# First image of a convolution and attention block: x loaded ahead of the raw taps, BatchNorm factors on VectorE, third buffer for the last output pieces

## The chip, the cores and the metric

One core of a Trainium2 chip runs the whole program. Its engines are named as in the profile: PE (TensorE, matrix products; PEld its weight loads), DVE (VectorE), ACT (ScalarE), POOL (GpSimd) and SP (SyncE, which here issues most of the DMA loads; POOL issues the stores). The metric is the device time of one execution in microseconds (us). A time within the program is given from the start of the profiled span.

## The reference

The input x has 8 images of 512 channels by 32 x 32 points, in 32-bit floats. Each image is normalised over 32 groups of channels, goes through a block, and is added to the block's output:

```python
def cbs(x, w, p, pad):
    return silu(bn_eval(conv2d(x, w, pad), p))     # bn: (x - m) * g / sqrt(v + 1e-3) + b

t = cbs(gn(x), cv1_w, cv1_bn, 0)                   # 512 -> 512, 1 x 1
ys = [t[:, :C], t[:, C:]]                          # C = 256
for i in range(2):
    yi = ys[-1]
    z = cbs(yi, m_cv1_w[i], m_cv1_bn[i], 1)        # 256 -> 256, 3 x 3
    z = bot_attention(z, m_qkv_w[i], m_rw[i], m_rh[i])   # 4 heads of 64 over 1024 points
    z = silu(bn_eval(conv2d(z, m_cv2_w[i], 0), m_cv2_bn[i]))
    ys.append(yi + z)
out = x + cbs(concat(ys, axis=1), cv2_w, cv2_bn, 0)
```

## The kernel before

Channels lie on the 128 partitions, in chunks of 128; the 1024 points of an image lie along the free axis and are worked on in two halves of 512. The images go one after another. From the second image on, the normalisation and cv1 of an image are done beside the attention of the image before it. The first image has nothing to hide behind: the part of the program ahead of the loop over `b` (L1271 to L1324) prepares it, and this is where most of the change lies.

That part does the following. SP's queue loads, in this order, chunk 0 of x, the raw 3 x 3 taps of the first convolution for output chunk 0 and input chunk 0 (`load_raw`, L153), chunk 1 of x, the first half of cv1's weights, chunks 2 and 3 of x, the second half of those weights, and then further raw taps and the BatchNorm parameters `bnp` (L205).

DVE takes statistics of the four chunks of x (`gn_stats`, L486 to L490). The group norm is made for chunks 0 and 1 and for chunks 2 and 3 apart (`group_norm_part`, L520): two small products on PE average over groups (`gm_ps`, `gv_ps`, L497), DVE makes the deviation (L506 to L509) and adds epsilon (L516), POOL raises to the power -0.5 and makes the shift (L517, L532, L533), and ACT applies scale and shift to x in place (L537). As chunks of x become ready, PE runs the products of cv1 (L387). Its four output chunks are taken in the order `Y_ORDER` = 2, 3, 0, 1; those of `ypad` (2 and 3) are the input of the first 3 x 3 convolution.

The 3 x 3 convolution is done by transforms: rows and columns of the input are transformed into `v_in` (`tiles_in`, L392 to L446, on DVE), the taps into `u` (`make_u`, L322 to L346, on DVE with copies on ACT), PE multiplies (L971), and DVE and ACT transform back (`columns_out`, L450; `rows_out`, L459). There are three transforms `i` = 0, 1, 2 of the taps for every pair of output chunk and input chunk `k`. For the first image the taps' transforms are made from the raw taps and also stored to memory for later images (L1318, L1268).

The factors of all BatchNorms are made in one go from `bnp`, 16 columns a partition: `rstd` = (variance + epsilon) to the power -0.5, `sh` = weight times `rstd`, `bh` = bias minus mean times `sh`, and two columns pairs of `sh` scaled by -1/12 (L1304 to L1311). All of this runs on POOL. Every SiLU (L370, on ACT) reads `sh` and `bh`.

The order of instructions on an engine is made when the program is built: a scheduler places each instruction by its own estimates of when its inputs are ready and by the order in the source. `tc.issue_after(ins)` asks that what is recorded inside it is not placed before `ins`. Each engine works through its list strictly in order.

At the end of the program, `cv2` (L1206) makes the last image's output, chunk by chunk. An output piece is a tile `t`: DVE adds an earlier partial product to PE's result (L1236), ACT applies SiLU, DVE adds the input x (L1239), and a DMA stores it (L1241). The last output chunk is cut into pieces of 512, 256 and 256 points, whose tiles have the tags "t", "h", "h"; each tag is a ring of two buffers, shared with other tiles of that tag. The tag "wt" is that of temporary tiles in `tiles_in` (L427).

Of the kernel before, what the change touches and what calls it, by code (L numbers as in the profile page):

```python
# [44 lines left out]
F32 = mybir.dt.float32  # L45
I32 = mybir.dt.int32
AF = mybir.ActivationFunctionType
ALU = mybir.AluOpType
# [4 lines left out]
P = 128  # L53
BN_EPS = 1e-3
# [7 lines left out]
def kernel(  # L62
# [16 lines left out]
    nc = tc.nc  # L79
# [4 lines left out]
    NX = C1 // P  # L84
    NM = C // P
# [12 lines left out]
    act = fast.enter_context(tc.tile_pool(name="act", bufs=1))  # L98


    def load_x(pool, b, c, bufs):
        xt = pool.tile([P, HW], F32, tag="x", name="x", bufs=bufs)
        src = x[b, ts(c, P), :] if isinstance(b, int) else x[bass.ds(b, 1), ts(c, P), :][0]
        nc.sync.dma_start(xt, src)
        return xt

    xs = [load_x(act, 0, 0, NX)]


    def ring(shape, name):  # L110
# [9 lines left out]
    def load_w1_half(i):  # L120
        ks = slice(i * NX // 2, (i + 1) * NX // 2)
        nc.sync.dma_start(w1[:, ks], cv1_w.rearrange("(k p) o -> p k o", p=P)[:, ks])
# [13 lines left out]
    def load_raw(n, oc, k, tag, bufs=1):  # L136
        raw = act.tile([P, 9, P], F32, tag=tag, name="raw", bufs=bufs)
        nc.sync.dma_start(raw, m_cv1_w[n, ts(k, P), :, ts(oc, P)])
        return rows_of_raw(raw)
# [11 lines left out]
        return rows_of_raw(raw[:, 0:9]), (both, mid)  # L151

    raws = {(0, 0, 0): load_raw(0, 0, 0, "k")}  # L153
    xs.append(load_x(act, 0, 1, NX))
    load_w1_half(0)
    xs += [load_x(act, 0, c, NX) for c in range(NX // 2, NX)]

# [40 lines left out]
    bnp = const.tile([P, NBN, 4], F32, name="bnp")  # L198
# [108 lines left out]
    sh = const.tile([P, NBN], F32, name="sh")  # L307
    bh = const.tile([P, NBN], F32, name="bh")
    rstd = const.tile([P, NBN], F32, name="rstd")
# [6 lines left out]
    def new_u(name):  # L316
        return ring([P, NM, 2, NC, P], name)
# [4 lines left out]
    def make_u(i, u, raw):  # L322


        rows, g1 = raw
        g0, g2 = rows[:, 0], rows[:, 1]
        stt, tt = nc.vector.scalar_tensor_tensor, nc.vector.tensor_tensor
        a, b = u[:, 0, 0:3], u[:, 1, 0:3]
        plus, minus = u[:, :, 1], u[:, :, 3]
        if i == 2:  # L330
            nc.scalar.copy(u[:, :, 0:3:2], rows[:, :, 0::2])
            tt(minus, rows[:, :, 0], rows[:, :, 2], ALU.add)
            tt(plus, minus, rows[:, :, 1], ALU.add)
            return tt(minus, minus, rows[:, :, 1], ALU.subtract)
        if i == 0:
            tt(b, g0, g2, ALU.add)
            tt(a, b, g1, ALU.add)
            tt(b, b, g1, ALU.subtract)
        else:
            stt(b, g2, 4.0, g0, ALU.mult, ALU.add)  # L340
            stt(a, g1, 2.0, b, ALU.mult, ALU.add)
            stt(b, g1, -2.0, b, ALU.mult, ALU.add)

        tt(minus, u[:, :, 0], u[:, :, 2], ALU.add)
        tt(plus, minus, plus, ALU.add)
        return stt(minus, minus, 2.0, plus, ALU.mult, ALU.subtract)  # L346
# [18 lines left out]
    def stages(act, small, ps_big, ps_av, n_pt):  # L365


        def silu(dst, src, k):

            return nc.scalar.activation(dst, src, AF.Silu, scale=sh[:, k : k + 1], bias=bh[:, k : k + 1])  # L370
# [635 lines left out]
        def cv2_products(w2, ys, oc, ks, ps=None, ends=None, by_half=False):  # L1006
            def cat(k, half):
                part, c = divmod(k, NM)
                if part in (1, 2):
                    return inner(ys[part], c, half)  # L1010
                return ys[part][:, c, ts(half, HALF)]

            nk = (2 + N) * NM
            return conv1x1(lambda k: w2[2 * k // nk][:, k % (nk // 2), ts(oc, P)], cat, nk, ks, ps, ends, by_half)
# [191 lines left out]
        def cv2(b, w2, ys, begun={}, parts={}):  # L1206

            def rows_of(dram, oc, at, n):  # L1210
                if isinstance(b, int):
                    return dram[b, ts(oc, P), at : at + n]
                return dram[bass.ds(b, 1), ts(oc, P), at : at + n][0]

            def residual(oc):
                t = act.tile([P, HW], F32, tag="xr", name="x_res", bufs=2)
                nc.gpsimd.dma_start(t, rows_of(x, oc, 0, HW))
                return t

            res = [residual(oc) for oc in range(2)]  # L1220
            for oc in range(NO):
                ks = range((2 + N) * NM)
                if oc in begun:
                    ps = cv2_products(w2, ys, oc, ks[-NM:], begun[oc], by_half=oc == NO - 1)
                else:
                    ks = ks[2 * NM if oc in parts else 0 :]
                    ps = cv2_products(w2, ys, oc, ks, ends=(ks[0], ks[-1]), by_half=oc == NO - 1)
                final = isinstance(b, int) and oc == NO - 1
                sizes = (HALF, HALF // 2, HALF // 2) if final else (HALF, HALF)
                x_res = res.pop(0)  # L1230
                at = 0
                for n, size in enumerate(sizes):
                    t = act.tile([P, size], F32, tag="h" if n and final else "t", name="t", bufs=2)
                    src = ps[:, at // HALF, at % HALF : at % HALF + size]
                    if oc in parts:
                        nc.vector.tensor_tensor(t, src, parts[oc][:, at : at + size], ALU.add)  # L1236
                        src = t
                    silu(t, src, bn_cv2 + oc)
                    nc.vector.tensor_tensor(t, t, x_res[:, at : at + size], ALU.add)  # L1239
                    q = nc.sync if final else nc.gpsimd  # L1240
                    q.dma_start(rows_of(out, oc, at, size), t)  # L1241
                    at += size
                if oc + 2 < NO:
                    res.append(residual(oc + 2))
# [26 lines left out]
    loaded = s.table_of(AF.Silu)  # L1271
    u_first = [new_u("u_new") for _ in range(PAIRS)]
# [3 lines left out]
    Y_ORDER = [*Y1S, *Y0S]  # L1276
    _, _, (_, read, _, _) = s.group_norm_part(xs[: NX // 2])
    norm = s.group_norm_part(xs[NX // 2 :])
    with tc.issue_after(loaded.ins):
        made = make_u(2, u_first[2][:, 0], raws[0, 0, 0])  # L1280
    with tc.issue_after(read.ins):
        next(norm)
    with tc.issue_after(made.ins):
        made = make_u(0, u_first[0][:, 0], raws[0, 0, 0])
    begun = {}

    def begin(oc, ks):
        begun[oc] = s.cv1_products(w1, xs, oc, ks, begun.get(oc))
        return s.last_product[0]
# [4 lines left out]
    with tc.issue_after(averaged.ins):  # L1294
        made = make_u(1, u_first[1][:, 0], raws[0, 0, 0])
    begin(Y_ORDER[0], [1])
    first = begin(Y_ORDER[1], [0])
    with tc.issue_after(first.ins):
        multiplied, _, applied, shifted = next(norm)
    with tc.issue_after(multiplied.ins):  # L1300
        begin(Y_ORDER[1], [1])
        begin(Y_ORDER[2], range(NX // 2))
    with tc.issue_after(shifted.ins):
        nc.gpsimd.tensor_scalar(rstd, bnp[:, :, 3], BN_EPS, None, ALU.add)  # L1304
        nc.gpsimd.tensor_tensor(rstd, rstd, mhalf[:, :NBN], ALU.pow)
        nc.gpsimd.tensor_tensor(sh, bnp[:, :, 0], rstd, ALU.mult)
        nc.gpsimd.tensor_tensor(bh, bnp[:, :, 2], sh, ALU.mult)
        nc.gpsimd.tensor_tensor(bh, bnp[:, :, 1], bh, ALU.subtract)

        for at in bn_m1:  # L1310
            nc.gpsimd.tensor_scalar(sh[:, at : at + NM], sh[:, at : at + NM], -1 / 12, None, ALU.mult)  # L1311
    with tc.issue_after(made.ins):
        made = make_u(0, u_first[0][:, 1], raws[0, 0, 1])
    with tc.issue_after(made.ins), tc.issue_after(applied.ins):
        for i in (1, 2):
            made = make_u(i, u_first[i][:, 1], raws[0, 0, 1])
    for i in range(PAIRS):
        nc.gpsimd.dma_start(u_dram[0][0][i], u_first[i])  # L1318
    last = made
# [6 lines left out]
    for b in range(B):  # L1326
# [6 lines left out]
        def u_of(n):  # L1333
            def of(oc):
                nonlocal last_load
                if b == 0 and n == 0 and oc == 1:
                    with tc.issue_after(last.ins):
                        for i in range(PAIRS):
                            make(n, oc, [i])
                got = [us.pop((oc, i)) if (oc, i) in us else load_u(n, oc, i) for i in range(PAIRS)]  # L1340
                if (b > 0 or n > 0) and oc == 1:
                    sq[n], last_load = load_sq(n)
                return got

            return of


        z, t = s.conv3x3(0, vs, u_of(0), b > 0)
# [4 lines left out]
        if more:  # L1353

            with tc.issue_after(last_load.ins) if last_load else nullcontext():
                xs = [load_x(act, b + 1, c, NX) for c in range(NX)]
# [60 lines left out]
        made = None  # L1417
        if b == 0:
            made = make(1, 1, [1], place=act.tile([P, NM, 2, NC, P], F32, tag="q", name="u_new"))
        with tc.issue_after(made.ins) if made else nullcontext():  # L1420
            last = s.m2(0, ao, y1, lambda oc, half: inner(y2, oc, half))
# [12 lines left out]
        z, t = s.conv3x3(1, vs, u_of(1), True)  # L1434
# [50 lines left out]
        last = s.m2(1, ao, y2, lambda oc, half: ylast[:, oc, ts(half, HALF)])  # L1485
# [103 lines left out]
```

## Time and profile before

| | us |
|---|---|
| median of 4 runs (lowest to highest) | 2319.03 (2318.39 to 2319.87) |
| the profiled execution: its own time | 2318.68 |
| the profiled execution: span from first to last instruction | 2317.2 |
| busy in the span: PE | 2288.7 (99%) |
| busy: DVE | 1838.6 (79%) |
| busy: ACT | 987.4 (43%) |
| busy: POOL | 94.7 (4%) |
| mean granted clock of PE | 0.997 |

A line of the timeline gives the start, the duration, the engine, the source line, the operation, the tile written and the tiles read, the sizes, how many instructions are merged, and in brackets the idle time of the engine before it and what released it. A line of the waits gives who waited for whom, the total, the number of waits and the longest. Instructions of DVE that do not depend on one another start before the one ahead has quite ended; so a stream of 128 x 256 operations advances by 0.34 us an operation, one of 128 x 384 by 0.47, although one alone takes 0.41 and 0.55. A PE product of 32-bit floats appears as two matmul records.

### The profile page before, as it was taken

To read this page: it belongs to the slowest core of one execution; us is meant where nothing else is said; L and a number is where in the kernel's file an instruction comes from. 1 tells how busy PE (TensorE), PEld (TensorE's weight loads), DVE (VectorE), ACT (ScalarE), POOL (GpSimd) and SP (SyncE) were. 2 spreads that over 40 slices of the span, in tenths; PEclk is the share of its full clock that TensorE was granted. 3 is DMA by queue.
4 is the path that set the end of the run, shared out by engine and by line. 5 is a ranking of instruction groups with operands and counts; after the bars stand their busy time and mean duration, and the time that the engine had idled before them with its cause. 6 is when DMAs were issued, how large, how long until landed. Compare 5 with 4: busy or idle time off the path is not lost.

```text
span 2317.2 us, 36534 instructions
## 1 busy us (share of the span) xinstructions
PE 2288.7 (99%) x14806; PEld 1174.2 (51%) x14806; DVE 1838.6 (79%) x2914; ACT 987.4 (43%) x1292; POOL 94.7 (4%) x314
## 2 busy tenths in 40 slices
PE   7999999999999999999999999999999999999998
PEld 4547346463554636446364553645436364473643
DVE  7887977888788887888788887888877988777774
ACT  2443624536144352544525345253542535335352
POOL 2000000000000000000000000000000000000000
PEclk9999999999999999999999999999999999999999
DMA  7422334041430415213151221602216031260201
GB/s 242 170 86 87 108 112 186 16 150 34 145 142 15 150 34 190 102 37 124 51 221 53 70 93 50 250 29 94 67 47 250 29 128 33 68 228 15 87 11 62
DMA packets 95521, 235.60 MB, mean 102 GB/s; under 512 B 28016, under 2 KB 50736, under 8 KB 81904
## 3 DMA queue, kind: packets, MB, share of 16 engines
q1 hardware_dynamic: 83600, 182.84, 23.5%
q0 software_dynamic: 11744, 50.34, 5.7%
q8 instruction: 119, 1.95, 0.4%
q14 instruction: 58, 0.48, 0.1%
HBM read 198.54 MB, written 34.60 MB: 101 GB/s over the span
## 4 chain that ended last, share of the span: by engine, by line
PE 96%; DVE 3%; POOL 0%; ACT 0%; DMA 0%; issue 0%; SPq 0%; DVEq 0%; POOLq 0%; ACTq 0%
PE av_ps L769 19%; PE l_ps L735 19%; PE c_ps L971 14%; PE c L1029 8%; PE p_ps L631 8%; PE x_ps L1141 6%; PE c_new L1029 6%; PE m_ps L995 5%; PE ps L387 4%; PE pv_ps L635 3%; PE s_ps L787 1%; PE p_ps L635 1%; PE s_ps L805 1%; DVE acc L755 0%; DMA raw<-in_m_cv_w_dram 0%; PE v_ps L596 0%
## 5 line engine op out<-in xcount | busy, mean ns | idle before, releaser
L739 ACT ACTIVATE pt<-l_ps 128x1024 f32<-128x1024 f32 x512 | 494.9, 1023 | 410.1 <-PE l_ps L735 385.6
L755 DVE TENSOR_TENSOR acc<-acc,pt 128x1024 f32<-128x1024 f32 x384 | 469.4, 1222 | 65.6 <-ACT pt L739 39.8
L769 PE MATMUL av_ps<-pt,vT 64*64 64x512 f32 x4096 | 486.5, 592 | 0.5 <-DVE ao L777 0.5
L735 PE MATMUL l_ps<-q,kr 64*64 64x512 f32 x4096 | 486.0, 590 | 0.0
L971 PEld LDWEIGHTS c_ps<-v_in,u 128*128 128x128 f32 x2720 | 306.0, 192 | 6.7 <-issue 6.7
L971 PE MATMUL c_ps<-v_in,u 128*128 128x128 f32 x2720 | 306.2, 275 | 0.0
L769 PEld LDWEIGHTS av_ps<-pt,vT 64*64 64x64 f32 x4096 | 159.2, 133 | 269.4 <-issue 224.3
L735 PEld LDWEIGHTS l_ps<-q,kr 64*64 64x64 f32 x4096 | 160.1, 133 | 263.3 <-issue 252.1
L453 ACT COPY m<-c_ps 128x256 f32<-128x256 f32 x96 | 35.4, 368 | 220.3 <-PE c_ps L971 214.9
L1029 PE MATMUL c_new<-t_in,ws 128*128 128x512 f32 x288 | 124.6, 592 | 0.0
L995 PE MATMUL m_ps<-ao,m_sb 128*128 128x512 f32 x256 | 112.5, 592 | 0.0
L370 ACT ACTIVATE m_kept<-m_kept,bh,sh 128x512 f32<-128x512 f32 x42 | 31.9, 806 | 146.0 <-DVE m_kept L1113 86.3
L753 DVE TENSOR_TENSOR acc<-pt 128x1024 f32<-128x1024 f32 x64 | 78.1, 1220 | 18.1 <-ACT pt L739 18.0
L1029 PEld LDWEIGHTS c_new<-t_in,ws 128*128 128x128 f32 x288 | 54.7, 190 | 68.9 <-issue 66.0
L631 PE MATMUL p_ps<-t_z,sq 128*128 128x512 f32 x180 | 87.1, 593 | 0.0
L370 ACT ACTIVATE t<-m_ps,bh,sh 128x512 f32<-128x512 f32 x64 | 48.0, 775 | 83.9 <-PE m_ps L995 82.5
L995 PEld LDWEIGHTS m_ps<-ao,m_sb 128*128 128x128 f32 x256 | 48.6, 190 | 61.2 <-issue 61.2
L1003 DVE TENSOR_TENSOR ylast<-t,ypad 128x512 f32<-128x512 f32 x32 | 22.0, 692 | 63.2 <-ACT t L370 63.2
L370 ACT ACTIVATE z<-z,bh,sh 128x512 f32<-128x512 f32 x64 | 48.6, 806 | 54.4 <-DVE z L482 54.4
L446 DVE TENSOR_TENSOR v_in<-w_rows 128x512 f32<-128x512 f32 x96 | 65.6, 683 | 0.0
L454 DVE TENSOR_TENSOR r_mid<-c_ps,m 128x256 f32<-128x256 f32 x64 | 27.1, 423 | 48.2 <-ACT m L453 48.1
L1029 PE MATMUL c<-ypad,ws 128*128 128x512 f32 x144 | 63.8, 592 | 0.0
(255 smaller groups left out, 3005.3 us busy)
## 6 DMA issues: line engine op xcount, KB each, us to landing
u<-u SPq DMA_DIRECT2D x85, 1024.0 KB
x<-in_x_dram SPq DMA_DIRECT2D x32, 512.0 KB
x_res<-in_x_dram POOLq DMA_DIRECT2D x32, 512.0 KB, 6.9
out_dram<-m_kept POOLq DMA_DIRECT2D x28, 512.0 KB, 7.5
u<-u_new POOLq DMA_DIRECT2D x12, 1024.0 KB, 5.2
w<-in_cv_w_dram SPq DMA_DIRECT2D x12, 1024.0 KB
rs<-r_dram SPq DMA_DIRECT2D x96, 128.0 KB
ws<-s SPq DMA_DIRECT2D x24, 512.0 KB
```

What stands on the lines that cost most here:

```text
L370: return nc.scalar.activation(dst, src, AF.Silu, scale=sh[:, k : k + 1], bias=bh[:, k : k + 1])
L387: last_product[0] = nc.tensor.matmul(ps[:, half, :], w_of(k), rhs_of(k, half), start=(k == begin), stop=(k == end))
L631: nc.tensor.matmul(ps[:, o, :], w[:, o, :], rhs, start=not onto, stop=True, skip_group_check=onto)
L635: nc.tensor.matmul(v[:, ts(j, P)], rhs[:, ts(j, P)], w[:, 2, :], start=j == 0 and not onto, stop=True, skip_group_check=True,)
L735: nc.tensor.matmul(ps[kh * HD : (kh + 1) * HD, hd, :], kr[r, c, o : o + HD], q[r, c, ts(half, HALF)], start=True, stop=True,)
L739: exp = nc.scalar.activation(pt[:, i], ps, AF.Exp, scale=SCALE)
L755: ins = nc.vector.tensor_tensor(accs[g], accs[g], pt[:, i], ALU.add)
L769: nc.tensor.matmul(avs[g][hd * HD : (hd + 1) * HD, kh, :], vT[r, j, o : o + HD], pt[r, i, hd, :], start=(j == 0), stop=(j == NJ - 1),)
L971: nc.tensor.matmul(ps[:, row, col, :], us[i][:, k, row, SLOT[col], :], vs[i][:, k, row, col, :], start=(k == 0), stop=(k == NM - 1),)
L995: nc.tensor.matmul(pss[oc][:, half, :], m2_sb[:, n, k, ts(oc, P)], ao[:, k, ts(half, HALF)], start=(k == 0), stop=(k == NM - 1),)
L1029: nc.tensor.matmul(ps[:, o, :], w[:, k, ts(o, P)], rhs[part][:, c, :], start=(k == 0 and not onto), stop=(k == KB - 1), skip_group_check=onto,
L1141: nc.tensor.matmul(ps[:, o, :], w[:, c, ts(o, P)], rhs[c], start=(c == 0 and not onto), stop=(c == 1), skip_group_check=onto,)
```

## The change

Three things are changed. (1) Both of the first two chunks of x are loaded ahead of the raw taps, and the first tap transform made (`make_u(2, ...)`) is asked to stand behind the last DVE reading of the first half's norm (`read`). (2) Of the BatchNorm factors only the power stays on POOL; the addition of epsilon, the two products, the subtraction and the two scalings move to DVE, between tap transforms: the first behind `make_u(1, ...)` of input chunk 0, the others behind `make_u(0, ...)` of input chunk 1. (3) The tiles of the last three output pieces have the tags "h", "h", "wt".

```diff
-    xs = [load_x(act, 0, 0, NX)]
+    xs = [load_x(act, 0, c, NX) for c in range(NX // 2)]
...
     raws = {(0, 0, 0): load_raw(0, 0, 0, "k")}
-    xs.append(load_x(act, 0, 1, NX))
     load_w1_half(0)
...
-                    t = act.tile([P, size], F32, tag="h" if n and final else "t", name="t", bufs=2)
+                    t = act.tile([P, size], F32, tag=("h", "h", "wt")[n] if final else "t", name="t", bufs=2)
...
     norm = s.group_norm_part(xs[NX // 2 :])
-    with tc.issue_after(loaded.ins):
-        made = make_u(2, u_first[2][:, 0], raws[0, 0, 0])
     with tc.issue_after(read.ins):
+        with tc.issue_after(loaded.ins):
+            made = make_u(2, u_first[2][:, 0], raws[0, 0, 0])
         next(norm)
...
-    with tc.issue_after(shifted.ins):
-        nc.gpsimd.tensor_scalar(rstd, bnp[:, :, 3], BN_EPS, None, ALU.add)
+    with tc.issue_after(made.ins), tc.issue_after(shifted.ins):
+        nc.vector.tensor_scalar(rstd, bnp[:, :, 3], BN_EPS, None, ALU.add)
         nc.gpsimd.tensor_tensor(rstd, rstd, mhalf[:, :NBN], ALU.pow)
-        nc.gpsimd.tensor_tensor(sh, bnp[:, :, 0], rstd, ALU.mult)
-        nc.gpsimd.tensor_tensor(bh, bnp[:, :, 2], sh, ALU.mult)
-        nc.gpsimd.tensor_tensor(bh, bnp[:, :, 1], bh, ALU.subtract)
+        made = make_u(0, u_first[0][:, 1], raws[0, 0, 1])
+    with tc.issue_after(made.ins):
+        nc.vector.tensor_tensor(sh, bnp[:, :, 0], rstd, ALU.mult)
+        nc.vector.tensor_tensor(bh, bnp[:, :, 2], sh, ALU.mult)
+        nc.vector.tensor_tensor(bh, bnp[:, :, 1], bh, ALU.subtract)
 
         for at in bn_m1:
-            nc.gpsimd.tensor_scalar(sh[:, at : at + NM], sh[:, at : at + NM], -1 / 12, None, ALU.mult)
-    with tc.issue_after(made.ins):
-        made = make_u(0, u_first[0][:, 1], raws[0, 0, 1])
-    with tc.issue_after(made.ins), tc.issue_after(applied.ins):
+            last = nc.vector.tensor_scalar(sh[:, at : at + NM], sh[:, at : at + NM], -1 / 12, None, ALU.mult)
+    with tc.issue_after(last.ins), tc.issue_after(applied.ins):
         for i in (1, 2):
             made = make_u(i, u_first[i][:, 1], raws[0, 0, 1])
```

## The prediction

> **What bounds the kernel now.** I read the page first, then the tensor engine's (PE's) waits, then the timeline of the first 97 us and of the last 15, and last the granted clock in 4-us stretches. Times are us from the span's start. Line numbers are those of the kernel before.
>
> ```profile
> PE 2288.7 (99%) x14806; PEld 1174.2 (51%) x14806; DVE 1838.6 (79%) x2914; ACT 987.4 (43%) x1292; POOL 94.7 (4%) x314
> ```
>
> PE is busy 99% of the span, so only what makes PE wait or run slow is worth time. All of PE's waits:
>
> ```profile
> PE gm_ps L497 <- DVE mv L490: 11.0, 1, 11.0
> PE ps L387 <- ACT x L537: 2.7, 1, 2.7
> PE c_ps L971 <- DVE u_new L341: 2.4, 1, 2.4
> PE gv_ps L497 <- DVE dev L509: 0.9, 1, 0.9
> PE ps L387 <- ACT z L370: 0.9, 1, 0.9
> PE c_ps L971 <- DVE r_ends L457: 0.7, 1, 0.7
> PE c_ps L971 <- DVE u_new L345: 0.5, 1, 0.5
> PE av_ps L769 <- DVE ao L777: 0.5, 1, 0.5
> ```
>
> All lie in the first 116 us, so whatever the first image gains or loses there is carried unchanged to the end. The first image, in the order of time:
>
> ```profile
> 4.68 1.29 DVE L489 BATCH_NORM_STATS2 st<-x 128x6 f32<-128x512 f32 x2 [4.68 <-DMA x<-in_x_dram]
> 8.05 0.42 DVE L332 TENSOR_TENSOR u_new<-raw 128x256 f32<-128x256 f32 x1 [1.83 <-DMA raw<-in_m_cv_w_dram]
> ...
> 9.35 1.29 DVE L489 BATCH_NORM_STATS2 st<-x 128x6 f32<-128x512 f32 x2
> ...
> 15.44 5.21 PE L387 MATMUL ps<-x,w 128*128 128x512 f32 x6 [2.74 <-ACT x L537]
> ...
> 26.72 3.03 POOL L1305 TENSOR_TENSOR rstd<-rstd,mhalf 128x16 f32<-128x16 f32 x1
> ...
> 29.83 4.56 POOL L1306 TENSOR_TENSOR sh<-bnp,rstd 128x16 f32<-128x16 f32 x1
> ...
> 35.02 2.78 ACT L370 ACTIVATE ypad<-ps,bh,sh 128x512 f32<-128x512 f32 x4 [5.57 <-POOL bh L1308]
> ...
> 36.50 0.69 DVE L423 SCALAR_TENSOR_TENSOR w_tmp<-ypad 128x512 f32<-128x512 f32 x1 [2.19 <-ACT ypad L370]
> ```
>
> Two waits in series stand out. VectorE (DVE) reaches the second chunk's statistics only at 9.35, because three tap operations that waited for the raw taps stand before them; the first product of cv1 follows at 15.44. And the BatchNorm factors come off POOL so late (4.56 us for 16 elements a partition) that the first SiLU waits till 35.02 and the input tiles (L423) till 36.50. From 36.50 to 70.2 DVE is never idle; in that stretch PE waits for DVE, and its clock drops:
>
> ```profile
> 60.00:64.00 4.00, 1.56 (x12) 1.21 (x11) 4.00 (x12) 0.92 (x2) 0.00 (x0) 1.00 0.42 111
> 64.00:68.00 4.00, 2.82 (x11) 2.53 (x12) 4.00 (x12) 0.97 (x2) 0.26 (x1) 0.58 0.14 40
> 68.00:72.00 4.00, 4.00 (x23) 4.00 (x22) 2.71 (x8) 0.00 (x0) 0.80 (x2) 0.57 0.81 328
> ```
>
> (columns: length, busy PE, PEld, DVE, ACT, POOL, clock, DMA share, GB/s. A mean of 0.58 and 0.57 is half rate for 3.4 us of each stretch, so from about 64.6 to 71.4.)
>
> **The change, part by part.**
>
> *Both x chunks first.* The second x load passes one 576 KB load on SP's queue. Bound of its landing: 4.68 plus 524 KB at 410 GB/s (the DMA rate of 9 to 12 us) is 5.98, at 253 GB/s (the lowest rate between 4 and 6 us) 6.75. DVE is done with the first chunk at 6.13, so I take 6.13, nearest to the 4 KB rows' own rate. The DVE, PE and POOL steps that follow are those of before: 1.32 to the aggregate (9.35 to 10.67), 3.91 to the normalisation on ACT (10.67 to 14.58), in all 11.36. POOL's two small operations there may meet DVE's two-input ones: in the second half of the norm they took 0.33 and 0.53 us, against 0.19 and 0.23 in the first; so 11.36 to 11.8. I take 11.5. PE starts 0.86 later, 12.35 for 15.44.
>
> The raw taps land at 9.35 for 8.05 (one x load of 1.3 later). DVE comes for them at 9.68, after the last reading of the first norm, so that costs nothing; w1 and the later loads have the same bytes ahead of them as before. If the second half of x is as late as its statistics were (13.28 and 15.06), its aggregate is there at 16.87, still before PE asks for it (12.35 + 5.15 = 17.5). That is the cover of all DVE work put behind the first norm; 0.6 us of it is left.
>
> *PE to the second norm.* Six products, the second norm's two small ones: 15.44 to 23.90 (L516 reads the result), 8.46 us. Half of it runs at 0.85 us a matmul record, the rest at 0.43: PE starts slow for 4.8 us. With the same spell DVE reads at 20.81. A spell 1.5 us shorter or longer moves everything after by 0.75; I keep that for the range. The order of DVE's instructions has a new wait here: L516 stands three operations earlier, and four tap operations queue behind it. DVE would have reached it about 1.5 us sooner, so this wait, and not DVE's work, sets the time.
>
> *Factors.* DVE then needs 2.46 us for the rest of the third tap transform (22.16 to 24.77 less the 0.15 that L516 took), so the variance plus epsilon (now DVE, 0.16 like L516) comes at 23.38, its bnp loads long landed (no DMA moved from 20.0 to 24.5). POOL's power: 23.62 to 26.65, with the 3.03 us of L1305. Beside it DVE does the six operations that took 24.77 to 27.80, till 26.53. The new wait, DVE on POOL, costs 0.2. Five small operations (0.2 each where chained, 0.11 where not) end at 27.55. All else queued behind it: eleven tap operations, 5 x 0.47 + 6 x 0.34 = 4.39, so L423 could run at 31.94. Its input: PE finishes the first output chunk at 32.5 - 3.1 = 29.4, two SiLUs take 1.45, 30.9: in time. So the tiles start 4.56 us earlier, by a DVE that has left five tap operations (3 x 0.47 + 2 x 0.34 = 2.09) for later.
>
> For POOL's power the row is L1305: 3.03 us while DVE ran two-input operations with small gaps. The nearest row that speaks against it is L1306, which did not end until DVE fell idle at 34.3. Were the power held back in the same way, till DVE is through at 26.53, it would end at 29.6, 2.9 us more: the upper bound. Lower bound: 0.9 us (L517, 2 elements), which gains only the 0.2. I take L1305, the same operation on the same tile. The Trainium skill, "SBUF — State Buffer", section "SBUF: two separate sides", says that the port pair which DVE and GpSimd share is an exclusive lock, a DVE operation with two SBUF inputs among its holders, and the loser is fully blocked. By that rule the sum would be the upper bound, about 2317; the trace agrees for L1306 and not for L1305.
>
> *Tiles to the second output chunk.* The built order shows that the second k of the first tap transform for output chunk 1 now stands behind the first chunk's row sums. Before, DVE needed 26.78 us from L423 to the end of L482 (63.28), eleven tap operations of 4.26 us among it; to the same point the new order holds eleven of 4.39. The products need it up to L345, 1.0 before. So PE can go on with chunk 1 at 31.94 + 26.78 + 0.13 - 1.0 = 57.85. It has then 47 of its 48 products left (before: 26 at 66.83), 0.226 us each (14.68 / 65): 10.6 us. PE is ready at 46.2 - 3.1 + 10.8 = 53.9 and idles about 3.9 us, so the clock will drop as it did at 64. Before, 26 products took 8.09 us instead of 5.87, a loss of 2.2. Bounds of the loss now: 0, with DVE's next taps (5.1 us) and 32 products as a floor, 70.1; and 3.4, half of a slow spell of 6.8 us spent busy, 71.9. I take 2.4: 70.9 against 74.92.
>
> The Trainium skill, "TensorE: Matmul & The Clock Gate", section "Part 1", has the clock judged in free-running windows of 3.4 us, so that such spells differ from run to run; a first spell of 5.1 us on average would add 0.15 to the sum.
>
> *Third tile at the end.* Nothing:
>
> ```profile
> 2305.62 0.54 POOL L1241 DMA_DIRECT2D out_dram<-t  x1 [2.96 <-DVE t L1239]
> 2306.39 1.88 PE L387 MATMUL ps<-ylast,w 128*128 128x512 f32 x4
> 2308.31 0.69 DVE L1236 TENSOR_TENSOR t<-ps,part 128x512 f32<-128x512 f32 x1 [2.03 <-PE ps L387]
> ```
>
> The first piece waited for PE's last product (2308.27). The tile's old store was issued at 2305.62 and lands in 2.3 to 2.5 us, by 2308.1. Without it the piece starts at the same moment; the other two take buffers long free. Bound: 0 to 0.05 either way.
>
> **Sum.** 74.92 - 70.9 = 4.0 us, nothing lost later. The profiled execution took 2318.68 (span 2317.2, 1.5 around it), so 2314.7. It lies 0.35 under the median of the runs, 2319.03; I leave it there. 0.2% (4.64 us), about what a measurement of this kernel tells from no change, is 2314.39, so the forecast is a small gain just inside that line.
>
> **Rivals.**
> - *The clock is kinder*: the first slow spell is shorter by up to 1.5 us, or the idle 3.9 us falls across two windows and the second slow spell is missed. Gain 4.8 to 6.5: 2312.3 to 2313.9. For it: PE at 15.44 could have come earlier in its spell; against it: a shorter idle stretch dropped the clock before.
> - *POOL is shut out*: the power ends at 29.6, factors at 30.5, tiles at 34.9. Gain 1.1 to 2.2: 2316.5 to 2317.6. For it L1306, against it L1305.
> - *Swallowed*: x lands late, or the 47 products that are left eat the lead. Gain under 1: 2317.7 to 2319.
> - *Slower*: the idle 3.9 us leave PE at half rate for nearly all of chunk 1. At half rate throughout, 47 products take 21.2 us, 57.85 + 21.2 = 79.1, 4.1 later than before: 2322.8. It decides from a slow time of 12.9 us on (57.85 + 10.6 + 6.45 = 74.9). Against it: the spell of before ended after 6.8 us.
>
> **How the numbers follow.** Steps hold: 0.70, 2313.5 to 2316.2, of it 0.27 beyond 0.2%. Kinder clock 0.15, all beyond. POOL shut out 0.08, swallowed 0.03, slower 0.04. Faster 0.42, same 0.54, slower 0.04. The range reaches from the middle of the kind clock, 2312.9, to the middle of the shut-out case, 2317.0; some 0.15 is left out.
>
> **What would show it.** Right: the first product near 12.4, L516's second reading near 20.8, POOL's power of about 3 us, the first SiLU released by PE near 29.5 and not by POOL, L423 near 31.9, PE idle 3 to 4 us before 58, first attention product near 92.8 (before 96.84), the last pieces released by PE as now. Wrong: a power of over 4 us, a DVE idle before its sh operation, or PE slow for much longer than 7 us after its idle stretch.

## The result, and the profile after

The changed kernel takes 2313.81 us (median of 34 runs, 2312.61 to 2315.18), the kernel before 2318.89 (54 runs, 2317.23 to 2320.42). The ratio is 0.9979 with a 95% interval of 0.9974 to 0.9984: 5.08 us less, or 0.16 to 0.26%. The forecast was 2314.7 and a gain just inside 0.2%; the measured gain, 0.22%, lies just outside, with an interval that holds both. One execution of the changed kernel, in the comparison side by side below, took 8580.57 us and is left out of the figures there.

The profiled executions took 2318.68 and 2314.09 us, with spans of 2317.2 and 2312.6. Line numbers of the kernel after are lower by one than those of the kernel before, from L154 on, except between L1305 and L1314, where the lines of the factors were rewritten. First the waits of PE (who waited for whom, total us, times, longest):

```profile
PE gm_ps L496 <- DVE mv L489: 8.1, 1, 8.1
PE c_ps L970 <- DVE u_new L344: 3.2, 1, 3.2
PE ps L386 <- ACT x L536: 2.7, 1, 2.7
PE ps L386 <- ACT z L369: 0.9, 1, 0.9
PE gv_ps L496 <- DVE dev L508: 0.9, 1, 0.9
PE av_ps L768 <- DVE ao L776: 0.5, 1, 0.5
```

The first wait was 11.0, and the three waits in the second output chunk (2.4, 0.7 and 0.5) have become one of 3.2. The timeline of the kernel after:

```profile
6.38 1.29 DVE L488 BATCH_NORM_STATS2 st<-x 128x6 f32<-128x512 f32 x2 [0.40 <-DMA x<-in_x_dram]
...
9.85 0.42 DVE L331 TENSOR_TENSOR u_new<-raw 128x256 f32<-128x256 f32 x1
...
12.46 5.21 PE L386 MATMUL ps<-x,w 128*128 128x512 f32 x6 [2.72 <-ACT x L536]
...
20.91 0.16 DVE L515 TENSOR_SCALAR gr<-gv_ps 128x2 f32<-128x2 f32 x1 [1.77 <-PE gv_ps L496]
...
23.68 3.16 POOL L1304 TENSOR_TENSOR rstd<-rstd,mhalf 128x16 f32<-128x16 f32 x1 [0.55 <-DVE rstd L1303]
...
26.88 0.18 DVE L1307 TENSOR_TENSOR sh<-bnp,rstd 128x16 f32<-128x16 f32 x1 [0.25 <-POOL rstd L1304]
...
29.69 1.45 ACT L369 ACTIVATE ypad<-ps,bh,sh 128x512 f32<-128x512 f32 x2 [3.09 <-PE ps L386]
...
31.90 0.68 DVE L422 SCALAR_TENSOR_TENSOR w_tmp<-ypad 128x512 f32<-128x512 f32 x1
...
57.94 12.15 PE L970 MATMUL c_ps<-v_in,u_new 128*128 128x128 f32 x90 [3.17 <-DVE u_new L344]
...
91.86 3.66 PE L734 MATMUL l_ps<-q,kr 64*64 64x512 f32 x32
```

The second chunk's statistics start at 6.38 for 9.35, the raw taps are there when DVE comes for them (no wait at 9.85), the first product comes at 12.46 for 15.44, the first SiLU is released by PE at 29.69 and not by POOL at 35.02, the tiles start at 31.90 for 36.50, and the first attention product comes at 91.86 for 96.84. The lead at that point is 4.98 us, and nothing of it is lost up to the last output pieces (2303.27 for 2308.31, 5.04). The spans differ by 0.44 less, 4.6: from the first of the last pieces to the end it takes 9.33 us for 8.89. The granted clock in stretches of 4 us (columns as in the prediction) drops as it did before, but for less long: as in the prediction, 0.78 and 0.79 make half rate for about 3.4 us in all:

```profile
56.00:60.00 4.00, 2.04 (x9) 1.75 (x10) 4.00 (x11) 1.41 (x2) 0.53 (x1) 0.78 0.00 0
60.00:64.00 4.00, 4.00 (x30) 4.00 (x30) 4.00 (x12) 0.48 (x2) 0.12 (x1) 0.79 0.66 266
```

### The profile page after: what moved, and what is told of

Its sections match the earlier page's. It is cut to its first block, busy times and chain, and to the rows that moved or that the text cites. A ratio compares the mean times of both kernels' runs of the same rounds, so it can differ in the third digit from the quotient of the medians.

```text
span 2312.6 us, 36527 instructions
## 1 busy us (share of the span) xinstructions
PE 2287.0 (99%) x14806; PEld 1172.5 (51%) x14806; DVE 1840.1 (80%) x2920; ACT 987.7 (43%) x1292; POOL 89.0 (4%) x308
## 4 chain that ended last, share of the span: by engine, by line
PE 96%; DVE 3%; ACT 0%; DMA 0%; POOL 0%; issue 0%; SPq 0%; DVEq 0%; ACTq 0%
PE av_ps L768 19%; PE l_ps L734 19%; PE c_ps L970 14%; PE c L1028 8%; PE p_ps L630 8%; PE x_ps L1140 6%; PE c_new L1028 6%; PE m_ps L994 5%; PE ps L386 4%; PE pv_ps L634 3%; PE s_ps L786 1%; PE p_ps L634 1%; PE s_ps L804 1%; DVE acc L754 0%; PE v_ps L595 0%; DMA x<-in_x_dram 0%
```

## The experiments

Three theories stood at the start. The prediction's: the late start of PE and POOL's late factors are two waits in series, so both parts of the change are needed. Its rivals: the loads carry all of it, or the factors do. Each run is compared with runs of the kernel before on the same chip.

### The loads alone

```diff
-    xs = [load_x(act, 0, 0, NX)]
+    xs = [load_x(act, 0, c, NX) for c in range(NX // 2)]
...
-    xs.append(load_x(act, 0, 1, NX))
...
-    with tc.issue_after(loaded.ins):
-        made = make_u(2, u_first[2][:, 0], raws[0, 0, 0])
     with tc.issue_after(read.ins):
+        with tc.issue_after(loaded.ins):
+            made = make_u(2, u_first[2][:, 0], raws[0, 0, 0])
         next(norm)
```

> Only the first part of the change: both first chunks of x ahead of the raw taps, and the tap operations of pair 2 behind the first norm's last reading. BatchNorm's factors stay on POOL, the tiles at the end as before.
> Theory 1 (the prediction's: two waits in series, each worth its own part): the first product comes at 12.4, as in the whole change, and the second norm's reading near 20.9. But POOL's first product of the factors (4.56 us for 16 elements a partition in the profile of before) again does not end before DVE falls idle, near 31.4, the first SiLU is released by POOL at about 32 and not by PE at 29.7, and the input tiles start near 33.5, 3.0 earlier than before and 1.6 later than in the whole change. Gain about 3 us, between 2.5 and 4 by how long the tensor engine runs at half clock later: 2315 to 2316.5.
> Theory 2 (the loads carry all of it, POOL's factors are hidden once PE is earlier): the first SiLU is released by PE near 29.7, tiles near 31.9, time that of the whole change, 2313.8.
> Theory 3 (the early start is swallowed by DVE's work): tiles not before 35.5, gain under 1 us.

Measured: 2312.59 us, before 2318.12; ratio 0.9976 (0.9966 to 0.9985), 5.5 us less. That is theory 2, the loads carry all of it, and theory 1 falls. Its timeline:

```profile
23.26 3.06 POOL L1304 TENSOR_TENSOR rstd<-rstd,mhalf 128x16 f32<-128x16 f32 x1
...
26.01 0.55 DVE L339 SCALAR_TENSOR_TENSOR u_new<-raw 128x384 f32<-128x384 f32 x1
...
26.39 0.25 POOL L1305 TENSOR_TENSOR sh<-bnp,rstd 128x16 f32<-128x16 f32 x1
...
26.72 0.28 POOL L1306 TENSOR_TENSOR bh<-bnp,sh 128x16 f32<-128x16 f32 x1
...
29.27 1.45 ACT L369 ACTIVATE ypad<-ps,bh,sh 128x512 f32<-128x512 f32 x2 [3.14 <-PE ps L386]
...
30.91 0.68 DVE L422 SCALAR_TENSOR_TENSOR w_tmp<-ypad 128x512 f32<-128x512 f32 x1
```

POOL's product that took 4.56 us in the kernel before takes 0.25 here, on the same tile and beside the same dense run of DVE operations. POOL's factors are ready by 28.4, in time for a SiLU that PE releases at 29.27, and the tiles start 1.0 us earlier than in the whole change. Half of that is a shorter first slow spell of PE in this execution (L515 at 20.44 for 20.91); the other half is that DVE has neither the small operations of the factors nor the wait for the power.

### The factors alone

```diff
-    with tc.issue_after(shifted.ins):
-        nc.gpsimd.tensor_scalar(rstd, bnp[:, :, 3], BN_EPS, None, ALU.add)
+    with tc.issue_after(made.ins), tc.issue_after(shifted.ins):
+        nc.vector.tensor_scalar(rstd, bnp[:, :, 3], BN_EPS, None, ALU.add)
         nc.gpsimd.tensor_tensor(rstd, rstd, mhalf[:, :NBN], ALU.pow)
-        nc.gpsimd.tensor_tensor(sh, bnp[:, :, 0], rstd, ALU.mult)
+        made = make_u(0, u_first[0][:, 1], raws[0, 0, 1])
+    with tc.issue_after(made.ins):
+        nc.vector.tensor_tensor(sh, bnp[:, :, 0], rstd, ALU.mult)
...
```

> Only the second part of the change: BatchNorm's epsilon, products and shifts on VectorE, only the power on POOL, and pair 0's second half beside the power. The loads and the tiles at the end as before.
> Theory 1 (two waits in series): the first product stays at 15.4, PE's first output chunk ends where it did, at 32.5, and releases the first SiLU then (before: POOL at 35.02), so the tiles start near 34.8 for 36.50, with some tap operations (1.3 us) left for later. Gain 0.4 to 1.7 us: 2317.2 to 2318.5, about 2318.0.
> Theory 2 (the factors were the bound and carry most of the gain): gain over 2.5 us, under 2316.4.
> Theory 3 (DVE takes the work off POOL and pays for it, its wait for the power among it): slower than before, 2319 to 2320.

Measured: 2316.63 us, before 2318.12; ratio 0.9994 (0.9985 to 1.0003), a gain of 1.5 us whose interval goes from 3.5 to a loss of 0.7. In the profile PE releases the first SiLU at 31.97, DVE stands 1.44 us for POOL's power, the tiles start at 35.00 (expected 34.8) and the first attention product comes at 95.34, 1.5 earlier than before. Part of this is again a shorter first slow spell in this execution (L516 at 23.20 for 23.90). So the factors may be worth something while PE starts late, as theory 1 had it, but the interval reaches zero. The two parts don't add up (5.5 and 1.5 against 5.1); the intervals are too wide to show that alone, but the profile of the loads alone does, since PE releases the first SiLU there without any help from the factors.

### The third tile alone

```diff
-                    t = act.tile([P, size], F32, tag="h" if n and final else "t", name="t", bufs=2)
+                    t = act.tile([P, size], F32, tag=("h", "h", "wt")[n] if final else "t", name="t", bufs=2)
```

> Only the third part: the three last output pieces take three tiles instead of two. All before the last output chunk is the kernel before.
> Theory 1 (the prediction's): nothing, 2318.9 within 0.3; the first of the last pieces starts 1.9 to 2.0 us after the last products began, released by PE as before.
> Theory 2 (the piece did wait for the old store): 0.1 to 0.7 us faster.
> Theory 3 (a loss at the end, since from the first piece to the span's end after took 9.3 us where before took 8.8): about 0.4 us slower, and the last stores on SP's queue take 2.8 us or so instead of 2.2.

Measured: 2318.73 us, before 2318.12; ratio 1.0002 (0.9993 to 1.0011). The interval goes from 1.6 us faster to 2.5 slower, so the times can't tell the three theories apart. The profile speaks against theory 2: the first of the last pieces was released by PE, 1.86 us after DVE's work before it, and not by the old store. For theory 3 the times are no help either. But every run of this study has a profile, and the stretch from the first of the last pieces to the span's end is 8.73 to 8.99 us in the six profiles with two tiles (mean 8.92) and 8.82 to 9.63 in the eight with three (mean 9.25). DVE's and ACT's steps there are the same to 0.02 us; the difference lies in the last stores (2.27 us on SP's queue against 2.61 on average). That points to a loss of 0.3 us from the third tile, by one execution each and with overlapping ranges; why it should be is open.

### The whole change with the products back on POOL

```diff
-        nc.vector.tensor_tensor(sh, bnp[:, :, 0], rstd, ALU.mult)
-        nc.vector.tensor_tensor(bh, bnp[:, :, 2], sh, ALU.mult)
-        nc.vector.tensor_tensor(bh, bnp[:, :, 1], bh, ALU.subtract)
+        nc.gpsimd.tensor_tensor(sh, bnp[:, :, 0], rstd, ALU.mult)
+        nc.gpsimd.tensor_tensor(bh, bnp[:, :, 2], sh, ALU.mult)
+        nc.gpsimd.tensor_tensor(bh, bnp[:, :, 1], bh, ALU.subtract)
...
```

> The whole change, but the products and shifts of BatchNorm's factors are back on POOL, behind its power; the epsilon is still added by DVE.
> Theory 1 (POOL's small two-input operation can't run beside DVE's dense two-input tap operations, as its 4.56 us in the profile of before suggest): the first product of the factors starts at 26.85 and ends only when DVE falls idle, near 31.4; the first SiLU is released by POOL at 32 or later, the tiles start 1 us or more later than 31.90; 2314.6 to 2315.2.
> Theory 2 (the 4.56 us were an accident of that place): the products take 0.2 to 0.5 each, are done by 28.5, the first SiLU is released by PE at 29.7, and the time is that of the whole change or some 0.3 less: 2313.4 to 2313.9.

Measured: 2312.40 us, before 2318.12; ratio 0.9974 (0.9964 to 0.9984), 5.7 less. Theory 2: the product starts at 26.49 and takes 0.26, the tiles start at 31.03, the first attention product comes at 90.26. Its line of the product:

```profile
26.49 0.26 POOL L1307 TENSOR_TENSOR sh<-bnp,rstd 128x16 f32<-128x16 f32 x1
```

So it isn't the length of POOL's chain that the change had to shorten.

What made the 4.56 us, then? In the kernel before, DVE's dense run of two-input tap operations (each starting before the one ahead of it has ended) begins at 27.80, and POOL's product comes at 29.83, 2.03 us into it. With the loads first, DVE waits for PE at L515 until POOL's chain starts too, and the product comes only 0.38 us into the run. The next two runs change that distance.

### Pair 1's taps earlier, factors on POOL

```diff
-    with tc.issue_after(averaged.ins):
+    with tc.issue_after(made.ins):
         made = make_u(1, u_first[1][:, 0], raws[0, 0, 0])
```

> The run with the loads alone, and one more edit: pair 1's first half is put behind pair 0's instead of behind the second norm's mean, so that DVE does three tap operations (1.5 us) in the 1.77 us in which it waited for the second norm's variance. BatchNorm's factors are on POOL, and its first product still starts near 26.4, but DVE's dense run of tap operations then begins near 24.5 instead of 26.0, so that POOL comes 1.9 us into it (in the profile of before 2.03 us into it, and it took 4.56; with the loads alone 0.38 us into it, and it took 0.25).
> Theory A (POOL is shut out when it first comes late into a dense run of DVE's two-input operations): the product lasts until DVE runs dry near 31, the first SiLU is released by POOL at 32 or later, and the time is no better than with the loads alone or up to 1.5 us worse: gain over before 4 to 5.5 us.
> Theory B (the 4.56 us had another cause): the product takes 0.2 to 0.5, the first SiLU is released by PE at 29.3, PE's waits in the second output chunk (2.5 us with the loads alone) shrink by about 1.5: gain 6.5 to 7.5 us.

Measured: 2315.09 us, before 2319.14; ratio 0.9984 (0.9975 to 0.9993), 4.05 less, so theory A. Its timeline:

```profile
23.75 0.55 DVE L339 SCALAR_TENSOR_TENSOR u_new<-raw 128x384 f32<-128x384 f32 x1
...
25.79 4.58 POOL L1305 TENSOR_TENSOR sh<-bnp,rstd 128x16 f32<-128x16 f32 x1
...
31.00 2.79 ACT L369 ACTIVATE ypad<-ps,bh,sh 128x512 f32<-128x512 f32 x4 [5.59 <-POOL bh L1307]
...
32.48 0.69 DVE L422 SCALAR_TENSOR_TENSOR w_tmp<-ypad 128x512 f32<-128x512 f32 x1 [2.21 <-ACT ypad L369]
```

The product comes 2.04 us into the run (which begins at 23.75), lasts 4.58, and ends at 30.37, 0.10 after DVE's last operation (32.48 - 2.21 = 30.27). The stall of the kernel before is back, and DVE then stands 2.21 us.

### The loads alone, with POOL's product delayed

```diff
         nc.gpsimd.tensor_tensor(rstd, rstd, mhalf[:, :NBN], ALU.pow)
+        nc.gpsimd.tensor_tensor(bh, rstd, mhalf[:, :NBN], ALU.pow)
```

> The run with the loads alone, with a second power of 16 columns on POOL (its result is not used) ahead of the factors' first product, so that this product starts near 29.55, 3.5 us into DVE's dense run, and 0.10 us before a DVE operation starts.
> Theory A (shut out when late): the product does not end before DVE runs dry near 31.0, so it takes 1.4 us or more for 0.25, the first SiLU comes at about 32.2 and the tiles at 33.7.
> Theory B (another cause): it takes 0.2 to 0.5, the SiLU comes at 30.9 and the tiles at 32.4.

Measured, in one execution: 2315.06 us, before 2319.14. The timeline has the second power and the product:

```profile
26.87 2.92 POOL L1305 TENSOR_TENSOR bh<-rstd,mhalf 128x16 f32<-128x16 f32 x1
...
29.76 1.74 POOL L1306 TENSOR_TENSOR sh<-bnp,rstd 128x16 f32<-128x16 f32 x1
...
32.14 2.12 ACT L369 ACTIVATE ypad<-ps,bh,sh 128x512 f32<-128x512 f32 x3 [5.53 <-POOL bh L1308]
...
33.62 0.69 DVE L422 SCALAR_TENSOR_TENSOR w_tmp<-ypad 128x512 f32<-128x512 f32 x1 [2.20 <-ACT ypad L369]
```

Theory A again: the product comes 3.28 us into the run (from 26.48) and ends at 31.50, when DVE has run dry (33.62 - 2.20 = 31.42). The figures expected for the SiLU (32.2) and the tiles (33.7) hold too. Only POOL's own chain was made longer here, so, by this one profile, the moment of its arrival is the cause, and not the operation.

### The whole change with pair 1's taps earlier

The edit is that of the run with the factors on POOL.

> The whole change, and the same further edit: pair 1's first half behind pair 0's instead of behind the second norm's mean. [...]
> DVE does 1.5 us of taps in its wait, the epsilon is added near 22, POOL's power ends near 26.0 instead of 26.84, DVE waits for it 0.9 instead of 0.25, and the tiles start near 31.1, where the first SiLU's end (29.7 + 1.45) holds them, for 31.90. PE's 3.2 us in the second output chunk become about 2.4, and the clock may hold: gain over the change 0.8 to 2 us, so 5.9 to 7 us over before.
> If POOL's part is what costs (theory A of the run before this), this one beats the loads with early taps by 1 us or more; if not (theory B), it is 0.5 to 1 us behind it, since DVE does five operations more and waits for the power.

Measured: 2314.91 us, before 2319.14; ratio 0.9985 (0.9976 to 0.9994), 4.2 less, no better than the change. POOL's part costs nothing here, but DVE now comes to the factors before POOL's power is done, and four more tap operations stand ahead of the tiles:

```profile
26.22 0.18 DVE L1307 TENSOR_TENSOR sh<-bnp,rstd 128x16 f32<-128x16 f32 x1 [1.44 <-POOL rstd L1304]
...
32.98 0.69 DVE L422 SCALAR_TENSOR_TENSOR w_tmp<-ypad 128x512 f32<-128x512 f32 x1
```

The expectation missed both: it had a wait of 0.9 and tiles at 31.1. PE then waited 2.8 and 0.5 us in the second output chunk and ran at half clock after.

### PE kept busy in its wait

Both kernels write six (or three) products of 128x512 into the second output chunk's first accumulator, which is started anew afterwards.

```diff
+                    for _ in range(warm.pop((oc, i), 0)):
+                        nc.tensor.matmul(
+                            ps[:, 0].rearrange("p c q -> p (c q)"), us_first[2][:, 0, 0, 0, :],
+                            vs[2][:, 0, 0].rearrange("p c q -> p (c q)"), start=True, stop=True,
+                        )
```

> The whole change, and six additional 128x512 products on PE ahead of the second output chunk (2.6 us at 0.43 each; the accumulator they write is started anew afterwards, so the result is the same). They fill most of the 3.17 us in which PE waited for the taps at 54.8, and add nothing to the path if they end by 57.94.
> Theory 1 (the idle 3.2 us made the clock drop to half for 3.4 us, which costs some 1.7 us): the granted clock stays at 1.00 from 56 to 64, the 90 products take 10.2 instead of 12.15, and the time is 1.2 to 1.9 us under that of the change: 6.3 to 7 us under before.
> Theory 2 (the slow spell costs nothing in the end, DVE's taps set the pace there): within 0.4 of the change.
> Theory 3 (the products run into the taps): up to 1 us slower than the change.

> The whole change, with three additional products on PE ahead of the second output chunk for six. With six, they took 5.32 us (two records of 0.43 each per product), the clock held at 1.00 and the end of the chunk was the same; so three take 2.6 us of the 3.17 in which PE waited, and end before the taps are there at 57.94.
> Theory 1 (the half clock costs 1.7 us of the change's time): clock 1.00 from 56 to 64, the 90 products take 10.2 to 10.5 for 12.15, the second chunk ends near 68.4; 1.2 to 1.9 us under the change, 6.2 to 7.0 under before.
> Theory 2 (DVE's taps set the pace in the chunk, not the clock): under 0.4 us from the change.

Measured: six products, 2313.76 us, before 2319.14, ratio 0.9978 (0.9969 to 0.9987); three products, 2313.29, before 2318.86, ratio 0.9975 (0.9965 to 0.9985). The first was mis-sized: a product is two records of 0.43 us, so that six took 5.32 us and ran past the taps. In the second the clock holds; in its windows and its PE timeline:

```profile
56.00:60.00 4.00, 3.12 (x18) 2.19 (x17) 4.00 (x12) 1.00 (x2) 0.40 (x1) 1.00 0.00 0
60.00:64.00 4.00, 3.82 (x33) 3.52 (x31) 4.00 (x12) 0.89 (x2) 0.13 (x1) 1.00 0.71 271
```

```profile
54.35 2.74 PE L969 MATMUL c_ps<-v_in,u_new 128*128 128x512 f32 x6
56.93 0.83 PE L976 MATMUL c_ps<-v_in,u_new 128*128 128x128 f32 x6
58.35 0.71 PE L976 MATMUL c_ps<-v_in,u_new 128*128 128x128 f32 x4 [0.59 <-DVE u_new L344]
59.35 3.84 PE L976 MATMUL c_ps<-v_in,u_new 128*128 128x128 f32 x32 [0.29 <-DVE u_new L345]
63.37 6.52 PE L976 MATMUL c_ps<-v_in,u_new 128*128 128x128 f32 x54 [0.18 <-DVE u_new L344]
```

And yet the chunk ends at 69.89, where the change had 70.09 (57.94 + 12.15). PE at full clock waits for DVE's taps three more times, 1.06 us in all. Theory 2, and the times agree: 2313.29 us beside 2313.34 for the change on the same chip (below). With PE at full clock DVE sets the pace here, so a slow PE spends in part time that it would have waited. This execution was 0.42 us later than the change's at the second norm (L515 at 21.33, counted as in the change, for 20.91), so by this count the half clock cost the change some 0.6 us in its first profile (70.09 - 20.91 = 49.18 us from the second norm to the chunk's end, for 69.89 - 21.33 = 48.56).

### The change and the loads alone, side by side

> The whole change once more, beside the next run on the same chip. 4.6 to 5.6 us under before.

> The loads alone once more, beside the whole change on the same chip. In the profiles DVE does five small operations fewer and never waits for POOL's power, the tiles start at 30.91 for 31.90, PE's longest wait in the second output chunk is 1.3 us for 3.2, its clock holds, and the first attention product comes at 90.14 for 91.86.
> Theory 1 (the factors on DVE cost time, since POOL isn't shut out there): 0.5 to 1.7 us under the whole change, 5.3 to 6.8 under before.
> Theory 2 (the better profile was a lucky one): the same as the whole change within 0.3 us.

Measured on one chip: the change 2313.34 us (nine runs; ratio 0.9976, 0.9966 to 0.9986), the loads alone 2312.53 (0.9974, 0.9963 to 0.9984), before 2318.86. The loads alone are 0.8 us under the change here. In the first comparison the change's ratio would make 2318.12 x 0.9979 = 2313.25, and the loads alone took 0.7 less, the products on POOL 0.9 less. The intervals overlap, so the times alone don't settle it; the profiles agree with theory 1, with the first attention product at 90.14 and 90.23 with the loads alone and at 90.26 with the products on POOL, for 91.86 and 91.65 in the two profiles of the change. In the second of these the first slow spell was shorter (six records in 4.29 us for 5.21), DVE came to L515 1.4 us earlier, and PE lost that to a longer second spell:

```profile
56.55 13.33 PE L970 MATMUL c_ps<-v_in,u_new 128*128 128x128 f32 x90 [3.16 <-DVE u_new L344]
```

It ends at 69.88, within 0.2 of the other. Its granted clock shows half rate for about 6.7 us, for 3.4 in the first:

```profile
56.00:60.00 4.00, 3.46 (x15) 3.38 (x16) 4.00 (x11) 1.52 (x2) 0.53 (x1) 0.50 0.31 131
60.00:64.00 4.00, 4.00 (x26) 4.00 (x25) 4.00 (x13) 0.37 (x1) 0.53 (x1) 0.66 0.48 182
```

Counted from the second norm as above (69.88 - 19.53 = 50.35 us for 48.56), the half clock cost 1.8 us here: how much DVE's pace hides depends on how long the slow spell lasts.

### Early taps without the wait for the power

The change with the early taps, and further:

```diff
-        made = make_u(0, u_first[0][:, 1], raws[0, 0, 1])
+        for i in (0, 1):
+            made = make_u(i, u_first[i][:, 1], raws[0, 0, 1])
     with tc.issue_after(made.ins):
...
-        for i in (1, 2):
-            made = make_u(i, u_first[i][:, 1], raws[0, 0, 1])
+        made = make_u(2, u_first[2][:, 1], raws[0, 0, 1])
```

> The whole change with the early taps, and pair 1's second half put with pair 0's ahead of BatchNorm's products, so that DVE no longer stands 1.44 us for POOL's power (it does six tap operations more first). DVE's idle time from 11.5 to 60 is then 1.2 us, for 3.1 in the change, 2.0 with the loads alone and 2.6 with the early taps before.
> Theory 1 (DVE's idle time before the second output chunk is what PE waits for there): PE's waits of 2.8 and 0.5 us fall to 1.8 or less in all and the half clock shrinks or goes; 1.5 to 3 us under the early taps before, 5.5 to 7 under before.
> Theory 2 (the early taps put the wrong taps first for PE, whatever DVE's idle time): PE still waits over 2.5 us at the second chunk with the clock at half after; 4 to 4.8 us under before.

Measured: 2311.34 us (6 runs), before 2318.86; ratio 0.9968 (0.9956 to 0.9979), 7.5 less, and 2.0 less than the change on the same chip. That is theory 1, at or beyond the upper end of its gain: PE's two waits in the second output chunk make 1.91 us, and the half clock is there but shorter, about 3.4 us for 6.8 with the early taps before. It is the fastest version here, though its interval overlaps that of the change (0.9966 to 0.9986). DVE's busy time between 11 and 60 us (fourth figure: length, PE, PEld, DVE) for the kernel before, the change and this one:

```profile
11.00:60.00 49.00, 45.31 (x204) 27.71 (x205) 42.31 (x109) 14.20 (x22) 15.29 (x25) 1.00 0.72 243
```

```profile
11.00:60.00 49.00, 44.35 (x183) 26.39 (x184) 45.26 (x118) 16.23 (x25) 8.50 (x18) 0.98 0.66 221
```

```profile
11.00:60.00 49.00, 46.12 (x210) 28.74 (x210) 47.29 (x125) 16.71 (x26) 8.34 (x18) 1.00 0.75 248
```

42.31, 45.26 and 47.29: DVE gained 2.95 us with the change and 2.03 more with this version, and the first attention product comes at 96.84, 91.86 and 90.09. DVE's busy time is not all that counts, though: the loads alone have only 45.89 in that stretch, five small operations fewer among it, and reach 90.14, with PE's clock held:

```profile
11.00:60.00 49.00, 46.54 (x208) 28.66 (x208) 45.89 (x115) 16.59 (x26) 10.31 (x23) 1.00 0.70 242
```

In this version two short waits of PE (0.81 and 1.10) still brought a slow spell:

```profile
58.67 0.71 PE L970 MATMUL c_ps<-v_in,u_new 128*128 128x128 f32 x4 [0.81 <-DVE u_new L340]
60.48 7.95 PE L970 MATMUL c_ps<-v_in,u_new 128*128 128x128 f32 x54 [1.10 <-DVE u_new L332]
```

```profile
60.00:64.00 4.00, 3.52 (x17) 3.52 (x18) 4.00 (x13) 0.00 (x0) 0.90 (x2) 0.58 0.53 197
64.00:68.00 4.00, 4.00 (x37) 4.00 (x37) 2.54 (x8) 0.37 (x1) 0.17 (x1) 0.99 1.03 393
```

## Why the prediction was right, and where it wasn't

- **Both x chunks first: right.** Predicted: normalisation on ACT at 11.5, first product at 12.35; measured 11.59 and 12.46. The second chunk landed 0.25 later than taken, inside its bounds (the lower of which should read 5.96, not 5.98), and the raw taps' delay was hidden as said. What the step did not say is that it is the whole gain.
- **PE to the second norm: right.** 20.81 predicted, 20.91 measured, with the slow spell repeated (5.21 us). The second profile of the change shows the other end that was kept for it: 4.29 us, and L515 at 19.53. The working has five tap operations queued behind L516, where the text says four; the sum has the time of all five.
- **Factors: right in every time, wrong in what they are worth.** The power took 3.16 us (3.03 taken), DVE's wait 0.25 (0.2), the last small operation ended at 27.55 (27.55 predicted). But "two waits in series stand out" took the 4.56 us of L1306 for a property of POOL beside DVE, which this part of the change would have to remove. It was one of arrival: the loads alone let POOL come early, it took 0.25, and the move to DVE then cost time (1.4 to 1.7 us at the first attention product; 0.7 to 0.9 in the medians, whose intervals overlap). The row itself held the hint, since L1305 ran through the start of the same dense run unhindered and only the operation that came later was shut out. That the sum came out all the same is luck: with this part or without it the first SiLU is released by PE, so a part that was taken as needed, and wasn't, left the total standing.
- **Tiles to the second output chunk: the mis-sized term.** PE resumed at 57.94 (57.85 predicted). But it had 45 products left and not 47 (90 records), 10.2 us at 0.226 each for 10.6; and these took 12.15, a loss of 2.0 where 2.4 was taken. So the chunk ended at 70.09 for 70.9. That this meets the floor given with the lower bound (70.1; its terms make 70.2) is chance: the floor goes with a loss of 0, and the clock did drop. The run with three more products puts the floor by DVE's taps some 0.6 us lower. The 0.8 us between 70.9 and 70.09 is most of what the first attention product came earlier than said (91.86 for 92.8).
- **Third tile: nothing at its front, as said** (PE released the piece), but the bound of 0.05 either way was too tight for the stores behind it: 0.44 between the two profiles, 0.3 between the groups of profiles. This took back part of what the term before had given, so two misses of opposite sign are in the time; hence 4.59 us between the profiled executions against the 4.0 of the sum.
- **Rivals.** POOL was not shut out of its power: 2.92 to 3.34 us in the profiles, and never to DVE's idling. Swallowed and slower did not come. The time, 2313.81, also lies in the span of "the clock is kinder", but the slow spells were there, so it isn't that case. In the change's second profile the first spell was 0.9 us shorter, but the second was twice as long, and the end of the chunk stayed where it was; two profiles don't tell whether that is chance.

## What to carry to other kernels

A stall's length belongs to the moment at which the instruction arrives, as much as to the instruction: before an operation is moved to another engine to get rid of a stall, ask whether another part of the change already alters when it arrives, and run that part alone. Where the bounding engine waits for a stream of work from another one, count that other engine's idle time up to that point (here 2.0 us more of DVE's work done by 60 us came with a first attention product 1.8 earlier, though the loads alone got there with less); where that stream sets the pace, a clock drop inside it costs less than the matmuls' own slowing (here 0.6 us of 2.0 in one profile, 1.8 of 3.2 in another).

## What the runs showed of the hardware

POOL's 16-column two-input product beside DVE's dense two-input operations: 0.25 and 0.26 us when it first came 0.38 or 0.39 us into the dense run (with the loads alone, both times, and with the products back on POOL), and 0.28 to 0.42 for the two after it, up to 1.1 us into the run; 4.56, 4.57, 4.58 and 1.74 us when it came 2.03, 2.03, 2.04 and 3.28 us into it (before, the third tile alone, early taps, delayed product), each time ending 0.08 to 0.10 after DVE fell idle. The Trainium skill, "SBUF — State Buffer", section "SBUF: two separate sides", says that whoever starts first has the shared ports for the whole instruction and the other is blocked; the four long cases agree that one side is blocked, but with the loads alone POOL got in between DVE's operations five times in a row, and in the kernel before not once in eleven. What decides between the two is open: the time into the run, having got in at its start, or the place within a DVE operation at which it comes (0.08 to 0.09 us ahead of the next one's start in the short cases; 0.04 ahead of one, or 0.03 behind one, in the long). No run here separates the three. POOL's power of 16 columns was never held up (2.92 to 3.34 us), nor DVE by it.

The clock dropped to half after a PE wait of 3.17 us, and also after two of 0.81 and 1.10 with 0.7 us of products between them; it held through waits of 0.95 and 1.32 that lay 4.3 us apart, with the loads alone:

```profile
56.22 4.31 PE L970 MATMUL c_ps<-v_in,u_new 128*128 128x128 f32 x32 [0.95 <-DVE u_new L345]
61.84 6.30 PE L970 MATMUL c_ps<-v_in,u_new 128*128 128x128 f32 x54 [1.32 <-DVE u_new L344]
```

```profile
56.00:60.00 4.00, 3.69 (x30) 3.50 (x30) 4.00 (x11) 1.77 (x3) 0.53 (x1) 1.00 0.65 260
60.00:64.00 4.00, 2.68 (x23) 2.45 (x22) 4.00 (x12) 0.00 (x0) 0.53 (x1) 1.00 0.62 182
```

The Trainium skill, "TensorE: Matmul & The Clock Gate", section "What's actually happening", gives one idle window of about 3.4 us as what takes the clock down; in the run with early taps and no wait for the power, 1.91 us of waits within 2.6 us were enough.
